# Unread identity products on TensorE, in nine places at both ends of a stack of four graph layers

## The chip, the cores and the metric

The kernel runs on one core of a Trainium2 chip. The core has five engines with their own instruction queues: TensorE (PE in the profile, with its weight loads shown apart as PEld), VectorE (DVE), ScalarE (ACT), GpSimd (POOL) and SyncE (SP), which here issues the transfers. Each engine works through its queue in order and waits on semaphores for the others. The metric is the device time of one execution in microseconds (us), lower is better.

## The reference

A batch of 32 graphs, each of 512 nodes with 256 features and a 0/1 adjacency matrix of 512x512, goes through four layers. After every layer comes a residual sum and a layer normalisation.

```python
x = _layernorm(x + layer0(x, adj))   # attention with 4 heads, relu, per-head normalisation
x = _layernorm(x + layer1(x, adj))   # attention with 1 head, elu
x = _layernorm(x + layer2(x, adj))   # transformer block: 8 heads, feed forward of 1024
x = _layernorm(x + layer3(x, adj))   # attention with 1 head, leaky relu

# a graph attention layer (3):
Wh = jnp.einsum('bnf,of->bno', h, W)
e = (Wh @ a1)[:, :, None] + (Wh @ a2)[:, None, :]
e = jnp.where(e > 0, e, ALPHA * e)
e = jnp.where(adj == 0, NEG_INF, e)
h_prime = jnp.einsum('bij,bjo->bio', jax.nn.softmax(e, axis=2), Wh)

# layer 2
scores = jnp.einsum('bhqd,bhkd->bhqk', q * scale, k)
attn = jax.nn.softmax(jnp.where(allowed[:, None], scores, -jnp.inf), axis=-1)
x = _layernorm(x + heads_joined(attn @ v) @ Wo.T + bo, ln1_g, ln1_b)
x = _layernorm(x + jax.nn.relu(x @ W1.T + b1) @ W2.T + b2, ln2_g, ln2_b)
```

## The kernel before

All 512 nodes of a graph lie as 4 rows of 128 partitions (R = 4, P = 128); the 256 features are 2 blocks of 128 (K = 2). Every layer is a Python generator that hands back control with `yield` between small pieces of work, called units here: one unit is, for example, the transposes of one feature block, the projection of one row, or the products of one attention row. `paced` (line 111) drives the generator of a stage and gives every unit a due time from the table `PLACES`, plus 12054 (`PERIOD`) times the graph's number. `graph` strings the stages of one graph together, and a merge of the 32 graphs by due time (line 832) sets the order in which the units are written out. So units of graph 0 stand beside units of graph 1, and in the steady part about four graphs are in work at once.

On TensorE this order is taken as written (`manual_schedule` for PE, line 831). For DVE, ACT and SP the framework's planner sets the order when the program is built: it goes through the instructions with estimates of their durations, hands out the buffers and banks that are free, and adds the waits.

All results of TensorE go to one pool of 8 PSUM banks (`bank`, in the pool `ps`), each 128x512 in float32. A bank is free again once it was read. Buffers named `part` (9 of them in stage "a") hold gb, pt and scratch tensors.

The units that matter here, with the names of the profile:
- layer 0: h0p (projection), gp (transposed broadcast of exponentials, copied to gb by ACT, line 349), then for each of four j: four pt on DVE (line 407), o and den on PE; then back on ACT (464), backp on PE, and a chain of DVE and ACT operations (lines 493 to 496, 293 to 302, and `layernorm`, lines 273 to 280) that ends with y on ACT (line 280).
- layer 1: xt1p (transposes of y, line 318 on), xt on ACT (line 320), h1p (projection), gp, gb, four pt, o in four rows, each by `attend`.
- layer 2: xt2p, qkp, hi (ACT, line 559) and lo (DVE, line 560), which are spread over partitions by transfers (line 567); s and pr, cp, den, ct (line 611), the projection wop, then a normalisation, ytp, f1p, ft (ACT, line 706), f2p, and two normalisations.
- layer 3: xt3p, h3p, gp, gb, pt, o in four rows, and the last normalisation.

Every matrix product is recorded by the helper `product`, so all have line 104 in the profile, and are told apart by their tensors. Between the units the kernel has no work for PE beyond what the merge places there; at the start only graph 0 and then graph 1 are under way, and at the end only graphs 30 and 31.

In weight preparation, `weights_ff` adds a loaded vector ln1b on DVE (line 227). The transfers of weights are issued on SP in the first 27 us.

The tensor `identb`, a bfloat16 identity of 128x128, is there already: it is multiplied with the mask `shut` in the products s<-shut,identb.

Of the kernel before, what the change touches and what calls it, by code (L numbers as in the profile page):

```python
# [44 lines left out]
        39499, 39646, 39646, 40873, 41200, 41449, 41464,  # L45
    ],
    "layer 3": [44919, 44919, 44969, 44969, 44969, 44969, 45682, 48065, 48065, 48065, 48422, 48422],
}
STAGES = {"edges": "a", "x": "a", "layer 0": "a", "layer 1": "a", "feed forward": "c", "layer 3": "c"}
ALL = mybir.DependencyInfo(mybir.DependencyClass.Sync, mybir.DependencyReason.DATA)  # L50
# [6 lines left out]
def tile_gnn_stack(tc: tile.TileContext, a: dict, out: bass.AP):  # L57

    nc = tc.nc
    with tc.tile_pool(name="verdict", bufs=1) as pool:
        bad = pool.tile([1, 1], I32, name="bad")
        fast_path(tc, a, out, bad)
        failed = nc.values_load(bad[0:1, 0:1])
        with tc.If(failed > 0):
            general_path(tc, a, out)
# [3 lines left out]
def fast_path(ctx: ExitStack, tc: tile.TileContext, a: dict, out: bass.AP, bad: bass.AP):  # L73
# [8 lines left out]
    nc = tc.nc  # L82
    B, N, D = a["x"].shape
    P = 128
    R = N // P
    K = D // P
    H, _, HO = a["w0"].shape
# [15 lines left out]
    def product(what, *args, **kwargs):  # L103
        latest[0] = what(*args, **kwargs).ins.name  # L104

    def in_place(op):

        if latest[0]:
            tc.add_manual_dep(op.ins, latest[0], ALL, reason="in its place")

    def paced(b, name, units):

        i = 0
        while True:
            stage[0] = STAGES.get(name, "b")
            try:
                next(units)
            except StopIteration as end:
                return end.value
            yield PERIOD * b + PLACES[name][min(i, len(PLACES[name]) - 1)]  # L120
            i += 1
# [4 lines left out]
    identb = const.tile([P, P], BF16, name="identb")  # L126
# [126 lines left out]
    def bank(name, dtype=F32):  # L253
        shape = [P, 2048 // (2 if dtype == BF16 else 4)]
        return ps.tile(shape, dtype, tag="mm", name=name, bufs=8)
# [546 lines left out]
    def graph(b):  # L802
        yield PERIOD * b + PLACES["edges"][0]
        rd = sb.tile([P, ND], F32, tag="rd", name="rd", bufs=3)
        mvs = sb.tile([P, 2 * NL * R + H * R + 2 * K], F32, tag="mvs", name="mvs", bufs=3)
        mv = [mvs[:, 2 * i * R : 2 * (i + 1) * R].rearrange("p (r s) -> p r s", s=2) for i in range(NL)]
        tops = mvs[:, 2 * NL * R :]
        var, spread = tops[:, : H * R], tops[:, H * R :]
        rds = [rd[:, ends[i] : ends[i + 1]] for i in range(3)]
        if b == 0:  # L810
            xt, x = yield from paced(b, "x", load_x(b))
        at = yield from paced(b, "edges", mask(b))
        if b:
            xt, x = yield from paced(b, "x", load_x(b))
        x = yield from paced(b, "layer 0", layer0_all(b, x, xt, at, rds[0], mv, var))
        x = yield from paced(b, "layer 1", layer1_all(b, x, at, rds[1], mv))
        a2 = yield from paced(b, "mask", symmetric(b, at))
        qk = yield from paced(b, "qkv", qkv_all(b, x))
        ct = yield from paced(b, "attention", attention(qk, *a2, spread))
        y = yield from paced(b, "projection", attended_all(b, x, ct))  # L820
        x = yield from paced(b, "feed forward", feed_forward_all(b, x, y, mv))
        x = yield from paced(b, "layer 3", layer3_all(b, x, at, rds[2], mv))
        nc.sync.dma_start(out[b].rearrange("(r p) d -> p r d", p=P), x)
        okd, oks, okv = ok[:, :ND], ok[:, ND : ND + NL * R], ok[:, ND + NL * R :]
        nc.vector.scalar_tensor_tensor(okd, rd, RD_MIN, okd, op0=ALU.is_ge, op1=ALU.mult)
        nc.vector.scalar_tensor_tensor(okd, rd, RD_MAX, okd, op0=ALU.is_le, op1=ALU.mult)
        variances = mvs[:, 1 : 2 * NL * R : 2]
        nc.vector.scalar_tensor_tensor(oks, variances, VAR_MAX, oks, op0=ALU.is_le, op1=ALU.mult)
        nc.vector.scalar_tensor_tensor(okv, tops, VAR_MAX, okv, op0=ALU.is_le, op1=ALU.mult)
# [12 lines left out]
    p = bank("badp")  # L842
# [651 lines left out]
```

## Time and profile before

| | |
|---|---|
| median of 3 runs | 3497.07 us (3495.69 to 3497.55) |
| profiled execution: its time | 3497.4 us |
| profiled execution: its span | 3495.6 us |
| mean granted clock of TensorE over the span | 0.986 |
| PE busy | 3397.5 us (97%) |
| PEld busy | 2366.5 us (68%) |
| DVE busy | 2888.4 us (83%) |
| ACT busy | 2223.0 us (64%) |
| POOL busy | 82.0 us (2%) |

Busy time is the time in which an engine executes, as the profiler records it; the ends of matrix products are modelled, so records of neighbours overlap, and the distance from start to start says what one costs in a row. The granted clock is the share of full speed at which TensorE was clocked; the profile gives it for every stretch of time. A group of instructions is written as out<-in with partitions x elements; "mean" is the duration of one. A float32 product shows two records in PE's timeline: a product of 256 float32 columns is two passes.

PE's waits and the chain of waits name the instruction that ended a wait last.

### The profile page before, as it was taken

Reading aid. Unit: us, or ns where it says so; the run is one execution under the profiler, and the core shown is the slowest. Engines: PE = TensorE matmul, PEld = TensorE weight load, DVE = VectorE, ACT = ScalarE, POOL = GpSimd, SP = SyncE. Lnnn points to the kernel's source line nnn. Section 1 sums busy time; section 2 is a strip of 40 time slices with the busy share of each in tenths; the row PEclk is TensorE's granted clock in tenths of the full one; section 3 lists DMA queues with packets and bytes.
Section 4 is the critical chain, followed back from the end, with each engine's and each line's share of the span. In section 5 each row is a group of like instructions: output and inputs, shape, how many; then the busy total and the mean of one; then the engine's idle time right before and its main releaser. Section 6 shows DMA issues by size and latency. Waiting matters only on the chain.

```text
span 3495.6 us, 51507 instructions
## 1 busy us (share of the span) xinstructions
PE 3397.5 (97%) x18342; PEld 2366.5 (68%) x18342; DVE 2888.4 (83%) x5178; ACT 2223.0 (64%) x5729; POOL 82.0 (2%) x171
## 2 busy tenths in 40 slices
PE   5799999999999999999999999999999999999986
PEld 3466667776667776667776667776666776666765
DVE  5778888888888888889888889888889888889863
ACT  3556667666667666667666667666667666666652
POOL 0000000000000000000000000000000000000000
PEclk8899999999999999999999999999999999999998
DMA  4334232333232333232333232334332333332220
GB/s 131 85 76 91 61 85 59 81 79 91 62 84 61 79 79 91 64 85 61 76 79 91 67 82 63 74 79 91 69 80 66 71 79 91 71 79 61 45 55 13
DMA packets 164038, 261.01 MB, mean 75 GB/s; under 512 B 20416, under 2 KB 56384, under 8 KB 163776
## 3 DMA queue, kind: packets, MB, share of 16 engines
q1 hardware_dynamic: 163776, 257.65, 32.0%
q8 instruction: 148, 2.42, 0.3%
q14 instruction: 114, 0.93, 0.1%
HBM read 106.57 MB, written 16.78 MB: 35 GB/s over the span
## 4 chain that ended last, share of the span: by engine, by line
PE 94%; DVE 3%; ACT 1%; issue 1%; DMA 1%; SPq 0%; POOL 0%; DVEq 0%; ACTq 0%; POOLq 0%
PE o L104 20%; PE f2p L104 13%; PE f1p L104 13%; PE s L104 8%; PE qkp L104 6%; PE cp L104 6%; PE den L104 5%; PE h3p L104 4%; PE wop L104 3%; PE h1p L104 3%; PE vp L104 3%; PE h0p L104 3%; PE gp L104 2%; PE backp L104 1%; PE xt3p L104 1%
## 5 line engine op out<-in xcount | busy, mean ns | idle before, releaser
L636 DVE TENSOR_TENSOR pr<-pr,a 128x1024 f32<-128x1024 f32 x384 | 454.7, 1217 | 185.4 <-ACT pr L633 185.4
L407 DVE SCALAR_TENSOR_TENSOR pt<-gb,ex,at 128x512 f32<-128x512 f32 x768 | 536.7, 742 | 42.0 <-ACT gb L349 31.6
L633 ACT ACTIVATE pr<-s 128x512 f32<-128x512 f32 x1024 | 545.3, 616 | 3.0 <-PE s L104 3.0
L104 PE MATMUL f2p<-wf,ft 128*128 128x256 f32 x2048 | 484.8, 379 | 5.4 <-ACT ft L706 5.2
L104 PE MATMUL f1p<-yt,wf 128*128 128x256 f32 x2048 | 483.8, 379 | 0.0
L104 PE MATMUL o<-h,pt 128*128 128x257 f32 x2048 | 476.5, 382 | 4.5 <-DVE pt L407 4.4
L104 PEld LDWEIGHTS o<-h,pt 128*128 128x128 f32 x2048 | 386.4, 190 | 99.1 <-issue 44.2
L663 DVE TENSOR_TENSOR pr<-pr 128x1024 f32<-128x1024 f32 x384 | 446.8, 1208 | 2.8 <-PE cp L104 2.8
L104 PEld LDWEIGHTS f2p<-wf,ft 128*128 128x128 f32 x2048 | 383.9, 190 | 63.4 <-ACT ft L706 9.8
L104 PEld LDWEIGHTS f1p<-yt,wf 128*128 128x128 f32 x2048 | 388.5, 190 | 55.0 <-DVE lo L560 0.5
L280 ACT ACTIVATE y<-y,rs 128x256 f32<-128x256 f32 x768 | 398.0, 593 | 17.1 <-DVE rs L276 17.1
L104 PE MATMUL s<-qk 128*128 128x512 f32 x1024 | 377.4, 470 | 4.6 <-DMA qk<-lo 3.8
L706 ACT ACTIVATE ft<-f1p,cols 128x256 f32<-128x256 f32 x512 | 217.0, 469 | 236.6 <-PE f1p L104 235.6
L273 DVE BATCH_NORM_STATS2 bn<-y 128x6 f32<-128x256 f32 x768 | 298.9, 410 | 5.6
L104 PE MATMUL o<-pt,hv 128*32 128x512 f32 x2048 | 286.5, 607 | 8.0 <-DVE pt L407 8.0
L265 ACT ACTIVATE rs<-mvs,eps1e-05_70 128x4 f32<-128x4 f32 x192 | 57.5, 300 | 326.7 <-DVE mvs L274 319.6
L104 PE MATMUL qkp<-xt,wqkv 128*128 128x512 f32 x512 | 240.5, 603 | 0.0
L104 PE MATMUL cp<-pr,v 128*32 128x512 f32 x2048 | 234.2, 595 | 1.4 <-DVE pr L636 1.4
L104 PEld LDWEIGHTS s<-qk 128*128 128x128 f32 x1024 | 189.3, 192 | 55.8 <-issue 27.7
L104 PEld LDWEIGHTS o<-pt,hv 128*32 128x32 f32 x2048 | 73.3, 110 | 179.6 <-issue 94.1
L559 ACT ACTIVATE hi<-qkp,cols 128x512 fp32r<-128x512 f32 x128 | 88.4, 691 | 164.1 <-PE qkp L104 162.1
L752 DVE RECIPROCAL rd<-o 128x1 f32<-128x1 f32 x128 | 21.5, 168 | 177.7 <-PE o L104 177.5
(139 smaller groups left out, 4881.9 us busy)
## 6 DMA issues: line engine op xcount, KB each, us to landing
qk<-hi SPq DMA_DIRECT2D x512, 128.0 KB, 3.4
qk<-lo SPq DMA_DIRECT2D x512, 128.0 KB, 3.5
adjt<-in_adjt SPq DMA_DIRECT2D x64, 512.0 KB, 3.9
adj<-in_adj SPq DMA_DIRECT2D x64, 512.0 KB, 5.0
xt<-in_xt SPq DMA_DIRECT2D x32, 512.0 KB, 3.8
x<-in_x SPq DMA_DIRECT2D x32, 512.0 KB, 5.1
out<-y SPq DMA_DIRECT2D x32, 512.0 KB, 4.5
wf<-in_w1t SPq DMA_DIRECT2D x1, 1024.0 KB, 9.8
```

Source lines behind the costliest of these rows:

```text
L104: latest[0] = what(*args, **kwargs).ins.name
L265: nc.scalar.activation(out, variance, AF.Ln, bias=eps[e])
L273: nc.vector.bn_stats(st[:, r, :], y[:, r, :])
L280: nc.scalar.activation(y[:, r, :], y[:, r, :], AF.Identity, bias=rs[:, 1, r : r + 1], scale=rs[:, 0, r : r + 1],)
L407: nc.vector.scalar_tensor_tensor(t, g, f, edges, op0=ALU.max, op1=ALU.mult)
L559: nc.scalar.activation(hi, p, AF.Identity, bias=bias)
L633: nc.scalar.activation(t[:, i, :], s, AF.Exp, scale=QSCALE)
L636: nc.vector.tensor_mul(t, t, edges)
L663: nc.vector.tensor_add(t, t, u)
L706: nc.scalar.activation(ft[:, f, :], p[:, f, :], AF.Relu, bias=bf1[:, ff + f : ff + f + 1])
L752: nc.vector.reciprocal(rd[:, r : r + 1], p[:, D : D + 1])
```

## The change

Before chosen units, `keep_busy` writes n products of `identb` with `identb` repeated four times, 128x512 in bfloat16, into a newly taken PSUM bank. Nothing reads the bank. The table `BUSY` is keyed by stage and unit (unit i is the piece that the i-th call of `next` runs, counted from 0), and then by graph: 0 and 1 are the first two, -2 and -1 the last two of the 32.

```diff
+BUSY = {
+    ("layer 0", 9): {0: 16, 1: 6},
+    ("layer 1", 1): {0: 72, 1: 40},
+    ("layer 1", 8): {0: 4},
+    ("layer 3", 1): {-2: 42, -1: 45},
+    ("projection", 1): {-1: 8},
+    ("layer 3", 8): {-1: 4},
+}
...
+    def keep_busy(n):
+        if n:
+            p = bank("busy").rearrange("p (r n) -> p r n", n=P)
+            for _ in range(n):
+                product(nc.tensor.matmul,
+                    p, identb, identb.unsqueeze(1).to_broadcast([P, R, P]), start=True, stop=True
+                )
+
     def paced(b, name, units):
 
         i = 0
         while True:
             stage[0] = STAGES.get(name, "b")
+            keep_busy(BUSY.get((name, i), {}).get(b if 2 * b < B else b - B, 0))
             try:
                 next(units)
```

Unit 9 of layer 0 is the first of the four j: its o products wait for pt. Unit 1 of layers 1 and 3 is the first block of transposes, xt1p or xt3p. Unit 8 of both is the first attention row, o. Unit 1 of the projection is the first row of wop. The products stand on PE directly ahead of these, 237 in all, in nine places; everything that follows on PE stands behind them.

## The prediction

> **What bounds the kernel now.** I read the slices of the page first, then the busy time per stretch, then PE's waits and PE's timeline at both ends, and last the granted clock in steps of 1 us.
>
> ```profile
> PE   5799999999999999999999999999999999999986
> PEclk8899999999999999999999999999999999999998
> ```
> ```profile
> 0.00:100.00 100.00, 64.50 (x324) 35.09 (x328) 58.77 (x100) 37.29 (x101) 4.68 (x16) 0.85 0.42 127
> 100.00:200.00 100.00, 79.68 (x408) 44.34 (x400) 73.14 (x113) 48.85 (x120) 2.96 (x5) 0.87 0.42 88
> ...
> 2000.00:2100.00 100.00, 100.00 (x552) 69.50 (x552) 86.61 (x159) 64.91 (x170) 2.49 (x5) 1.00 0.33 78
> ...
> 3400.00:3496.00 96.00, 66.70 (x274) 50.82 (x272) 31.96 (x93) 30.64 (x90) 0.00 (x0) 0.86 0.04 12
> ```
> The columns are stretch, length, busy us of PE, PEld, DVE, ACT and POOL, granted clock, DMA share, GB/s. From about 300 to 3300 us PE is busy without a break at clock 1.00: there the change can win nothing. But as that part is PE in a fixed order, every us by which PE reaches it earlier moves the end. The ends run at 0.85 to 0.87, and PE idles there. PE's waits of the first 250 us and from 3380 us on, each "waiter <- releaser: total, times, longest":
>
> ```profile
> PE xt1p L104 <- ACT y L280: 25.9, 2, 16.4
> PE o L104 <- DVE pt L407: 10.0, 6, 4.4
> ```
> ```profile
> PE xt3p L104 <- ACT y L280: 20.1, 2, 10.4
> PE wop L104 <- DVE ct L611: 2.5, 1, 2.5
> ```
> Four long waits are for a layer normalisation, a serial chain of DVE and ACT. After each of them PE works at half clock.
>
> **When the clock falls.** In steps of 1 us it changes at 19.56, 26.40, 43.46, 60.52, 67.36, 70.77, 84.42 and 87.84 us: the distances (6.84, 17.06, 17.06, 6.84, 3.41, 13.65, 3.42) are multiples of 3.41. So I cut the time into these windows:
>
> ```profile
> 57.11:60.52 3.41, 3.38 (x10) 2.19 (x11) 0.24 (x1) 1.98 (x4) 0.00 (x0) 0.50 0.00 0
> 60.52:63.94 3.42, 3.03 (x14) 2.28 (x12) 0.00 (x0) 1.47 (x4) 0.00 (x0) 1.00 0.00 0
> 63.94:67.36 3.42, 1.55 (x8) 1.00 (x8) 1.80 (x3) 0.91 (x4) 0.10 (x1) 1.00 0.00 0
> 67.36:70.77 3.41, 3.41 (x9) 2.47 (x8) 1.11 (x3) 0.75 (x2) 0.00 (x0) 0.50 0.00 0
> ...
> 118.54:121.96 3.42, 2.13 (x14) 0.53 (x16) 3.42 (x5) 2.42 (x5) 0.00 (x0) 1.00 0.89 173
> ...
> 139.03:142.44 3.41, 2.54 (x8) 1.29 (x7) 1.21 (x2) 3.41 (x8) 0.00 (x0) 0.50 0.00 0
> 142.44:145.86 3.42, 3.16 (x7) 2.52 (x8) 2.29 (x3) 1.06 (x3) 0.00 (x0) 0.50 0.01 2
> ```
> Each row decides the clock of the next. With 1.55 us of PE work (63.94) it falls, with 2.13 (118.54) it stays, with 3.38 (57.11) it rises; 2.54 us of transposes (139.03) do not raise it. [...]
>
> **The price of a product.** 237 bfloat16 products of 128x512 are added, each with its weight load. Nearest row: the pairs of an s product and a bfloat16 s<-shut of 128x512 take 0.46 us, and two s products alone also 0.46; so 0.23 us each at full clock. [...] The weight load (0.096 us on PEld) lies under the product before it. Each batch takes one of eight PSUM banks and is given back by PE itself: nothing, below by no more than one eviction (about 0.6 us, an ACT copy) for each of the nine batches, that is 0 to 5 us; I take 0, since in the waits the older banks are long read.
>
> **Place by place** (PE's timeline; PE is in order, so a product can only delay what follows it).
>
> *Graph 0, layer 0, 16 products* (3.5 us) in the 4.38 us before o at 21.04. PE then is warm and ends the first rows some 2 us earlier. But DVE's last four pt run at 32.95 to 35.7 behind the addition of ln1b, which waits for its DMA (landed 32.6, issued at 25.82, the queues full with weights). PE was already waiting for these pt. Gain 0; 2.4 at most if the addition gets another place in DVE's order.
>
> *Graph 0, layer 1, 72 products*: from 40.1 to 55.7 or 56.7. The last ACT y ends at 57.92, so the four transposes of k=0 end at about 58.1 in either case. The copies of xt (0.58 us) start at 58.3 and 58.84 instead of 58.49 and 59.34. h1p is 16 passes of 0.216 us warm (f1p: 8 in 1.73); seven pairs follow the second copy: 59.45 + 3.03 = 62.5 instead of 63.55. **1.0 us.**
>
> *Graph 0, layer 1, 4 products* (0.9 us) in the 1.55 us before o. The window holds 1.55 + 0.9 = 2.45 us and stays warm. The first row is paced by pt (0.68 us each, last ready at 68.3), ends at 68.8; three more of 1.73: 74.0 instead of 75.4. **1.3 us.**
>
> *Graph 1, layer 0, 6 products* (1.3 us) in the 2.19 us before 83.63: window 1.22 + 1.3 = 2.5. The last of four pt is ready at 85.5, o done at 85.9, den at 86.7 instead of 88.6. DVE's next pt waited 2.16 us for a buffer that den frees, so it moves too. **1.9 us.** The chain behind it (qkp, hi, the qk transfers, DVE from 113 to 137) hangs on PE and moves with it.
>
> *Graph 1, layer 1, 40 products* from 129.3, in 9.53 us. [...] The copies of xt stand behind four pr on ACT until 142.05, so xt1p may start as late as 141.0: 11.7 us of room. Then h1p warm: 3.46 instead of 5.31. **1.85 us.** If the cover were short, each 0.3 us of overrun costs 0.3.
>
> *Graph 30, layer 3, 42 products*: 9.1 to 9.7 us from 3386.85; the gap is 9.75, plus 1.4 up to the last y at 3398.02. h3p ends at 3402.4 instead of 3404.4. den and the ct of graph 31 stand behind it on PE: **2.0 us.** *Graph 31, projection, 8 products* (1.8 us) between den and wop, where PE waits 2.47 us for ct. wop x14 warm is 3.03 instead of 4.91: **1.9 us**; the o behind it (5.2 us) and ytp follow directly, and y's normalisation ends before them.
>
> *Graph 31, layer 3, 45 products*: 9.7 to 10.4 us in 10.36 plus 1.4. h3p ends 3.03 us after the second copy, which comes 0.1 earlier than 3469.43 + 0.58: 3472.4 instead of 3475.1. **2.7 us.** *The last 4 products* before o at 3477.4, where the clock was 1.00 already: 0; they keep it, should the window fall otherwise.
>
> Sum 1.0 + 1.3 + 1.9 + 1.85 + 2.0 + 1.9 + 2.7 = 12.7 us. Against it: between the end of the four long batches and h1p or h3p only transposes run for some 3 us. [...] By the rule a window lying in that stretch drops the clock, and the gain of the place is gone; I put it at one in four for each of four places: 0.25 x (1.0 + 1.85 + 2.0 + 2.7) = 1.9. By the busy rows alone it would be 0. I take it: **gain 10.8 us.** The profiled execution took 3497.4 (span 3495.6), the median is 3497.07, so 3486.6 and 3486.3: **3486.5 us.** What a measurement of this kernel can tell from no change is about 0.2%, 7.0 us.
>
> **The rivals.**
> *The clock falls again* at all four long waits. Left are 1.3 + 1.9 + 1.9 = 5.1 us: 3492, within 0.2%. For it: the transposes. Against it: their bursts are short, and a window must lie just so.
>
> *The order of the other engines shifts.* PE's order is written down, that of DVE, ACT and SP is made when the program is built, with the added products in its reckoning. In the steady part DVE is busy 85%; if one wait like that of o for pt at 172.0 (0.63 us) came back in each of some 30 graphs, 19 us are lost and 10.8 gained: 3505, slower. It decides from 0.36 us a graph on. For it: all graphs share buffers and banks, and nine more banks are handed out. Against it: the steady part has no wait now, DVE has 15 us of slack in 100, and nothing is added there.
>
> [...]
>
> **How the numbers follow.** Forecast 0.60 (its own range 3481 to 3490), clock falls again 0.20, order shifts 0.15, cold 0.05. Slower gets 0.12 of the shifted order and the cold 0.05: 0.17. Same gets 0.18 of the fallen clock and 0.03 of the shifted order: 0.21. Faster gets the forecast and 0.02 of the fallen clock: 0.62. Range 3480 (12.7 + 2.4 and some) to 3499 (5 us of bank waits or a small shift, set against the small gain): outside it are the cold case, most of the shifted order and a few hundredths below.
>
> **What would show it.** Clock 1.00 through 44 to 90 us and 3388 to 3475; h1p and h3p means near 390 ns instead of 435 to 557; PE's wait for y reduced to a rest; DVE's pt at 33 us still behind ln1b; the steady rows still 100.00. It is wrong if the rows between 300 and 3300 lose PE work, if busy products last over 0.23 us at clock 1.00, or if xt1p and xt3p start later than their y.

## The result, and the profile after

The kernel with the products takes 3490.23 us (median of 20 runs, 3488.44 to 3491.37); the kernel before, beside it, 3496.72 us (20 runs, 3493.08 to 3501.1). The ratio is 0.9981, with a 95% interval of 0.9974 to 0.9988: 6.5 us less, 0.19%. The forecast was 10.8 us less, 3486.5 us. The profiled execution took 3491.36 us, with a span of 3489.5 us (before: 3497.4 and 3495.6).

The 40 slices of the page, PE's busy share and the granted clock:

```profile
PE   7899999999999999999999999999999999999997
PEclk9999999999999999999999999999999999999999
```

Busy time per stretch, with the columns of the prediction (stretch, length, busy us of PE, PEld, DVE, ACT, POOL, granted clock, DMA share, GB/s):

```profile
0.00:100.00 100.00, 82.08 (x430) 42.40 (x434) 59.09 (x100) 37.40 (x101) 4.68 (x16) 0.98 0.42 128
100.00:200.00 100.00, 88.12 (x444) 47.68 (x440) 72.88 (x112) 48.87 (x120) 2.95 (x5) 0.93 0.42 87
2000.00:2100.00 100.00, 100.00 (x550) 69.52 (x549) 85.44 (x158) 65.57 (x172) 2.46 (x5) 1.00 0.33 80
3400.00:3489.00 89.00, 71.25 (x323) 50.90 (x321) 31.93 (x93) 29.70 (x85) 0.00 (x0) 0.97 0.04 13
```

The clock rose from 0.85, 0.87 and 0.86 to 0.98, 0.93 and 0.97 at the two ends; the middle is unchanged at 100.00 and 1.00. A higher mean clock is not yet time won: much of it lies over products that nobody reads, and what counts is how long the work behind each batch takes.

PE's waits of the first 250 us, and then from 3370 us on ("waiter <- releaser: total us, times, longest"):

```profile
PE xt1p L112 <- ACT y L297: 1.9, 7, 0.9
PE o L112 <- DVE pt L424: 5.9, 7, 2.2
PE h1p L112 <- ACT xt L337: 1.9, 2, 1.6
```
```profile
PE xt3p L112 <- ACT y L297: 2.2, 8, 0.7
PE wop L112 <- DVE ct L628: 0.8, 1, 0.8
```

The waits for y, 25.9 and 20.1 us before, are filled down to a rest. Two lines are to be kept in mind: a wait of h1p for xt of 1.6 us, and one of o for pt of 2.2 us. Each turns out to hold a part of the missing gain.

The batches and the work behind them in PE's timeline of after (start, us, operation, count, idle time before and what ended it):

```profile
42.17 15.70 PE L112 MATMUL busy<-identb 128*128 128x512 bf16 x72
61.23 3.81 PE L112 MATMUL h1p<-w1g,xt 128*128 128x258 f32 x16 [0.24 <-ACT xt L337]
...
127.21 10.49 PE L112 MATMUL busy<-identb 128*128 128x512 bf16 x40
141.68 5.16 PE L112 MATMUL h1p<-w1g,xt 128*128 128x258 f32 x16 [1.64 <-ACT xt L337]
...
3397.81 3.81 PE L112 MATMUL h3p<-w3g,xt 128*128 128x258 f32 x16 [0.24 <-ACT xt L337]
3406.30 3.29 PE L112 MATMUL wop<-wo,ct 128*128 128x256 f32 x14 [0.84 <-DVE ct L628]
3464.64 3.81 PE L112 MATMUL h3p<-w3g,xt 128*128 128x258 f32 x16 [0.24 <-ACT xt L337]
```

The same groups in PE's timeline of before:

```profile
59.12 4.43 PE L104 MATMUL h1p<-w1g,xt 128*128 128x258 f32 x16
...
142.70 5.30 PE L104 MATMUL h1p<-w1g,xt 128*128 128x258 f32 x16 [1.07 <-ACT xt L320]
...
3399.22 5.19 PE L104 MATMUL h3p<-w3g,xt 128*128 128x258 f32 x16
3409.09 4.91 PE L104 MATMUL wop<-wo,ct 128*128 128x256 f32 x14 [2.47 <-DVE ct L611]
3469.21 6.02 PE L104 MATMUL h3p<-w3g,xt 128*128 128x258 f32 x16
```

A projection that records 3.81 us ran warm (clock 1.00, its passes 0.22 us apart from start to start), one of over 5 us cold for most of its length (clock 0.50, 0.43 us apart); for the 14 passes of wop it is 3.29 against 4.91. Graph 0 and the whole tail are warm now (3.81, 3.81, 3.29, 3.81). Graph 1 is not: 5.16 against 5.30.

**Where the time went**, from the starts of the same instructions in both profiles. The first h0p starts at 10.54 instead of 9.16, and backp at 40.70 instead of 38.46: the kernel is 2.24 us *later* before any long batch begins. Behind that point the places give back 0.75 (graph 0, layer 1), 1.25 (its 4 products), 1.2 (graph 1, layer 0), 0.15 (graph 1, layer 1), 1.55 and 1.6 (the h3p of graph 30 and the wop of graph 31), and 2.4 (the h3p of graph 31), and the 3200 us between head and tail drift by 0.1: 9.0 us in all. 9.0 - 2.24 = 6.8 us, and PE's last product (badp) starts 6.78 us earlier, at 3480.72. The span is only 6.1 us shorter, since from the issue of the last output transfer to the end it takes 6.7 us instead of 6.0.

One place that neither kernel fills has a part in every such comparison. Ahead of the h3p of graph 29 (start 3310.55 in before, 3309.32 in after) PE waits 1.4 us for y, and in ten of the fourteen profiles of this case, before and after among them, the clock is at a half there for 3.41 us; in four (without products, half the products, bf1p moved, the addition alone) it is not. That is worth about 1.1 us.

In order of instructions ACT and POOL have the same as before, PE the same apart from the products. DVE differs in one place: one of the last pt of graph 0, layer 0, now stands ahead of the addition of ln1b.

Three things were open: why graph 1's h1p stayed cold, what the late start of the first 40 us is, and which batches earn their place.

### The profile page after: what moved, and what is told of

Its sections match the earlier page's. It is cut to its first block, busy times and chain, and to the rows that moved or that the text cites. A ratio compares the mean times of both kernels' runs of the same rounds, so it can differ in the third digit from the quotient of the medians.

```text
span 3489.5 us, 51983 instructions
## 1 busy us (share of the span) xinstructions
PE 3436.7 (98%) x18579; PEld 2383.9 (68%) x18579; DVE 2889.2 (83%) x5178; ACT 2222.6 (64%) x5729; POOL 81.7 (2%) x171
## 4 chain that ended last, share of the span: by engine, by line
PE 94%; DVE 3%; ACT 1%; issue 1%; DMA 1%; SPq 0%; POOL 0%; ACTq 0%; DVEq 0%; POOLq 0%
PE o L112 20%; PE f2p L112 13%; PE f1p L112 13%; PE s L112 8%; PE qkp L112 6%; PE cp L112 6%; PE den L112 5%; PE h3p L112 3%; PE h1p L112 3%; PE wop L112 3%; PE vp L112 3%; PE h0p L112 3%; PE gp L112 2%; PE backp L112 1%; PE xt3p L112 1%
```

## The experiments

Theory and rivals to begin with: the gain is the sum of the warm projections, about 3 us at the head and 6 at the tail, less what the start loses (theory); or head and tail are of another size than the profile says, because the head's loss belongs to the products and the tail's gain to luck (rivals). Every ratio is against "before", run in the same group. The intervals are some 3 us to either side, so a difference of 1 or 2 us between two changed kernels is not shown by the times alone. Line numbers shift a little between kernels.

**Head and tail apart.** One kernel keeps the batches of graphs 0 and 1 (138 products), the other those of graphs 30 and 31 (99).

```diff
 # head only
     ("layer 1", 8): {0: 4},
-    ("layer 3", 1): {-2: 42, -1: 45},
-    ("projection", 1): {-1: 8},
-    ("layer 3", 8): {-1: 4},
```
```diff
 # tail only
-    ("layer 0", 9): {0: 16, 1: 6},
-    ("layer 1", 1): {0: 72, 1: 40},
-    ("layer 1", 8): {0: 4},
     ("layer 3", 1): {-2: 42, -1: 45},
```

> Only the five batches of graphs 0 and 1 (138 products); the four of graphs 30 and 31 are left out. Theory (gain is where the clock no longer falls, and adds up): the two profiles give the head 1.15 us net, after 3.45 us won at xt1p, o and den of graphs 0 and 1 and 2.24 lost ahead of backp, of which 1.38 were already there at the first product and may be chance; so 1 to 2.5 us under before, 3494 to 3496. Rival (the start of the profile before was a lucky one, and the head wins all of 3.45 and more): 3.5 to 5 us under before.

> Only the four batches of graphs 30 and 31 (99 products). Theory: h3p of graph 30 1.55, wop 1.6, h3p of graph 31 2.4, together 5.6 us under before: 3491. Rival (the tail overlaps with DVE and part of it is taken back in the last normalisation): under 3.5 us.

Measured: head 3495.58 us (13 runs) against 3496.52, ratio 0.9994 (0.9986 to 1.0003); tail 3492.48 us (21 runs), ratio 0.9989 (0.9982 to 0.9995). So 0.9 and 4.0 us, together 4.9 where the change has 6.5; the intervals allow the two to add up. The head's interval includes no change at all; it excludes a gain of 5 us. The tail, costed at 6.6 us in the prediction before the discount, is under the 5.55 us that the profile of after shows. Its own profile shows what may be missing: there the h3p of graph 31 took 5.44 us, not 3.81. The same batch, with the same work behind it, is warm in one execution and cold in another.

**The addition of ln1b on GpSimd.** In after, PE waits 2.23 us for a pt on DVE, and that pt stands behind the addition, which waits for its transfer:

```profile
34.66 0.42 DVE L244 TENSOR_TENSOR b_b<-b_b,ln1b 128x256 f32<-128x256 f32 x1 [2.20 <-DMA ln1b<-in_ln1b]
```
```profile
35.80 2.78 PE L112 MATMUL o<-pt,hv 128*32 128x512 f32 x10 [2.23 <-DVE pt L424]
...
40.70 1.64 PE L112 MATMUL backp<-ident,back 128*128 128x128 f32 x12 [0.69 <-ACT back L481]
```

The first fence is DVE's timeline, the second PE's. The experiment takes the addition off DVE, so that no pt stands behind the transfer.

```diff
         bcast(ln1b, "ln1b")
-        nc.vector.tensor_add(lnb2, lnb2, ln1b)
+        nc.gpsimd.tensor_add(lnb2, lnb2, ln1b)
```

> All 237 products, and the addition of ln1b moved from DVE's queue to GpSimd's. Theory (the first 16 products win nothing because DVE's last pt of graph 0 stand behind an addition that waits for a weight transfer): the wait of 2.2 us for pt goes, backp starts 2 to 3 us earlier against the first product, the time is 2 to 3 us under the changed kernel. Rival (the start as a whole is later because transfers landed later, the addition only shows it): within 1 us of the changed kernel, and another wait for a transfer ahead of backp.

Measured: 3488.84 us (13 runs), ratio 0.9977 (0.9968 to 0.9985): 1.4 us under the change by the medians, which the intervals of the two alone don't separate. PE's timeline shows the mechanism, though:

```profile
36.21 1.63 PE L112 MATMUL backp<-ident,back 128*128 128x128 f32 x12 [0.69 <-ACT back L481]
```

backp starts 26.15 us after the first h0p (10.06), in after 30.16 us. The wait for pt of 2.2 us is gone. That less than those 4 us reaches the end is in part the clock's doing: in this profile the h1p of graph 0 took 4.87, that of graph 1 6.74 and the h3p of graph 31 5.49 us.

**Seven products more, before h1p of graph 1.** In graph 1 the copies of xt stand behind four pr on ACT, as the prediction said; so PE ends its batch at 137.7 and has only eight transposes until h1p at 141.7, 4 us. Two windows of 3.41 us from the trace of after:

```profile
137.73:141.14 3.41, 1.75 (x8) 0.94 (x8) 0.92 (x1) 3.41 (x9) 0.00 (x0) 1.00 0.00 0
141.14:144.55 3.41, 2.87 (x7) 2.31 (x8) 2.58 (x3) 1.35 (x4) 0.00 (x0) 0.50 0.01 2
```

1.75 us of PE work, nearly all of it transposes, and the next window has 0.50. The edit fills the wait between the transposes and the projection:

```diff
     ("layer 1", 8): {0: 4},
+    ("layer 1", 3): {1: 7},
```

> All 237 products and 7 more in graph 1 between the transposes xt1p and the projection h1p, in the 1.64 us in which PE waits for xt. Theory (the 40 products are spent for nothing because the clock falls after them, in a window that holds only transposes and this wait): clock 1.00 through h1p, h1p 3.8 us instead of 5.2, 1.4 to 1.7 us under the changed kernel. Rival (the stretch is bound by the copies on ACT, not by the clock): no gain over 0.3 us.

Measured: 3488.52 us (14 runs), ratio 0.9976 (0.9968 to 0.9984), by the medians 1.7 us under the change, which the intervals again don't separate. PE's timeline:

```profile
139.69 1.67 PE L113 MATMUL busy<-identb 128*128 128x512 bf16 x7
141.49 3.81 PE L113 MATMUL h1p<-w1g,xt 128*128 128x258 f32 x16
```

h1p starts when it did (141.49 and 141.68) and takes 3.81 us. So most of the gain which the prediction had given to the 40 products needed these seven too. In five profiles with the 40 products and without these seven, h1p took 5.15 to 6.81 us, never 3.81.

**The products out again, and the change a second time**, one run each: is the late start due to the products, and does a second execution of the change look like the first?

```diff
-BUSY = {
-    ("layer 0", 9): {0: 16, 1: 6},
...
-}
+BUSY = {}
```

> The changed source with an empty table of batches: no product at all, the same instructions as the kernel before. One look at the start: in the two profiles without products in graphs 0 and 1 the first h0p began at 9.2 us, in the four with them at 10.1 to 10.5, because the transfer of a landed later. Theory (chance of the transfers' start): anywhere from 9 to 10.6. Rival (the longer program delays the first transfers): 9.1 to 9.4.

> The changed kernel once more, for a second profile. Theory (free windows): h3p of graph 31 and h1p of graph 0 are warm (3.8 us) in some executions and partly cold (5.4, and about 4.5) in others, h1p of graph 1 is cold always. First h0p: by chance anywhere from 9 to 10.6; by the rival 10 to 10.6.

Measured: 3495.95 us without, with h0p at 9.17 as before; 3491.49 us for the change, with h0p at 10.85 and backp at 41.35. The h1p of graph 0 and both h3p were warm again, the h1p of graph 1 cold again (6.80).

**Half the products** in the four long waits: 36, 20, 21 and 22 (the expectation has 23 for the last). If some activity anywhere in the wait is enough, half is as good as all.

```diff
-    ("layer 1", 1): {0: 72, 1: 40},
+    ("layer 1", 1): {0: 36, 1: 20},
...
-    ("layer 3", 1): {-2: 42, -1: 45},
+    ("layer 3", 1): {-2: 21, -1: 22},
```

> The four long batches cut to half (36, 20, 21, 23 products), the five short ones as in the change. Theory (a batch is worth something only if it reaches up to the next work, as the clock falls in any window left idle): the clock falls in all four long waits, xt1p, h1p, xt3p and h3p are cold again, the 0.75 + 1.55 + 2.4 us of these places are lost: 4 to 5 us over the changed kernel. Rival (the products keep the clock for longer than a window, half of them would do): within 1 us of the changed kernel.

Measured: 3493.03 us (12 runs), ratio 0.9995 (0.9986 to 1.0003), 2.8 us over the change by the medians, less than the 4 to 5 expected. PE's timeline:

```profile
40.26 7.93 PE L112 MATMUL busy<-identb 128*128 128x512 bf16 x36
56.83 2.81 PE L112 MATMUL xt1p<-ident,y 128*128 128x128 f32 x8 [8.64 <-ACT y L297]
...
3395.89 4.64 PE L112 MATMUL h3p<-w3g,xt 128*128 128x258 f32 x16
```

In this profile the clock fell in all four waits (53 to 63, 124 to 131 and again 138 to 145, 3391 to 3398, 3459 to 3466 us; the fall at 124 is before the batch), and rose again only while the projections ran: they took 4.64 to 5.43 us, between the cold and the warm time. (The times from 124 to 145 us and at 3391 are an estimate, from the steps of 3.41 us and from what ran there: 20 products in 6.02 us, h1p in 5.35, h3p in 4.64.) That "between" may be why the loss was smaller than expected; the profiled execution, 3490.70 us, is the fastest of the twelve, so it can't tell what the median lost. In this profile what counts is that the products reach up to the next work, not that there are some.

**Everything at once, and one product between transposes.** In the profile of the run with the addition on GpSimd, the stretch ahead of the cold h3p looks like this:

```profile
3458.86:3462.27 3.41, 2.35 (x11) 1.35 (x12) 0.00 (x0) 2.83 (x6) 0.00 (x0) 1.00 0.00 0
3462.27:3465.68 3.41, 3.41 (x9) 2.69 (x9) 0.00 (x0) 1.33 (x8) 0.00 (x0) 0.50 0.00 0
```

PE is recorded busy for 2.35 us, more than the 2.13 us with which the clock stayed up at 118.54 in the kernel before. But here much of it is transposes of 128x128 in float32. (The row holds the eight transposes, 1.76 us, and three passes of h3p.) If transposes count less than products, a product between them is what is missing. The kernel has the change, the addition on GpSimd, the seven products, and in the long waits one product after each of the first three transposes of the first feature block:

```diff
     ("layer 3", 8): {-1: 4},
+    ("layer 1", 3): {1: 7},
 }
+BETWEEN = {("layer 1", 1): (0, 1), ("layer 3", 1): (-2, -1)}
...
                 )
+                if spare[0] is not None and r < R - 1:
+                    keep_busy(1, spare[0])
             nc.scalar.copy(t[:, k, :], p)
```

> The change, the addition of ln1b on GpSimd, 7 products before h1p of graph 1, and one product after each of the first three transposes of xt1p and xt3p in the four long waits, where PE waits for y anyway. Theory (transposes alone let the clock fall): clock 1.00 from there through h1p and h3p of all four graphs in every profile; gains of ln1b (1.5) and of h1p of graph 1 (1.7) add up, and the cold h3p of graph 31 and h1p of graph 0 go too (1.6 and 0.7 in about half of the executions): 4 to 5 us under the changed kernel, 3485 to 3486.5. Rival (more products only delay the transposes): 3487 to 3489.

Measured: 3484.95 us (6 runs) against 3496.58, ratio 0.9966 (0.9954 to 0.9978): 11.6 us under before. All four projections took 3.81 us. The end of the last long wait in PE's timeline:

```profile
3457.63 0.33 PE L114 MATMUL xt3p<-ident,y 128*128 128x128 f32 x1 [0.65 <-ACT y L307]
3457.79 0.38 PE L114 MATMUL busy<-identb 128*128 128x512 bf16 x1
...
3459.10 0.77 PE L114 MATMUL xt3p<-ident,y 128*128 128x128 f32 x5
3460.10 3.81 PE L114 MATMUL h3p<-w3g,xt 128*128 128x258 f32 x16 [0.24 <-ACT xt L349]
```

The products stand in the 0.16 us in which PE waits for the next y, and cost the transposes nothing that can be seen. One profile can't show that the clock never falls there; behind the batches it did not in this one, nor in that of the kernel with bf1p moved below. No run has the products between the transposes alone: by the medians they are what is left of 5.3 us under the change after 1.4 and 1.7 for the other two edits.

**The first 16 products**, taken out alone, and left alone. By the prediction they are worth nothing, 2.4 us at most. One rival made them the cause of the late start (A), another gave them a gain that the late addition hides (B).

```diff
 # without them
-    ("layer 0", 9): {0: 16, 1: 6},
+    ("layer 0", 9): {1: 6},
```
```diff
 # they alone
-BUSY = {
-    ("layer 0", 9): {0: 16, 1: 6},
...
-}
+BUSY = {
+    ("layer 0", 9): {0: 16},
+}
```

> The change without its first batch (16 products ahead of o in graph 0). Theory (that batch wins nothing, as DVE's pt wait for the addition of ln1b and so for a transfer): within 0.7 us of the changed kernel. Rival A (the batch is what delays the first transfers): first h0p at 9.1 to 9.3 us instead of 10 to 10.8, 1 to 2 us under the changed kernel. Rival B (the batch works as intended): 2 to 3 us over it.

> Only the first batch of 16. One look at the start: by rival A of the run before the first h0p begins at 10 to 10.8 us, else at 9.1 to 9.3. backp comes 29.3 us after the first h0p in the kernel before and 30.2 in the changed one; by the theory 29 to 30.5 here, by rival B 26.5 to 27.5.

Measured without them: 3491.2 us (14 runs) against 3497.07, ratio 0.9981 (0.9973 to 0.9989), that of the change; this alone would leave room for 2 to 3 us. h0p starts at 10.86: A falls. backp comes 29.16 us after it, with them 30.16: no sign of B in these two. With them alone 3496.11 us in one run, h0p at 10.70 and backp 27.28 us later, where before has 29.30: neither the 29 to 30.5 of the theory nor quite nothing. One number goes with both. In this profile the transfer of ln1b had landed early by the kernel's own clock (the addition starts 22.22 us after h0p, in after 24.12), and then the earlier rows of o are worth something. The distance from the addition to backp is nearly fixed: 5.85 us in before, 5.86 without the 16, 5.06 with them alone, 5.07 in the head alone, and 6.04 in after, where the clock falls in the wait (half clock from 35 to 39 us). So in these profiles backp follows the landing of the transfer, and the 16 products move the distance by less than 1 us to either side.

**bf1p moved.** In before and in every kernel so far the clock also falls between 190 and 197 us (in before at 193.6), with PE busy without a break. There stand the 32 passes of bf1p, of one column each. They, and the load of their weights wf1, go into the long wait of graph 1, two products after each four passes; the batch there shrinks from 40 to 8 and 16 of these. The rest is the kernel above.

```diff
-    ("layer 1", 1): {0: 72, 1: 40},
+    ("layer 1", 1): {0: 72, 1: 8},
...
+            if (name, i, b) == ("layer 1", 1, 1):
+                bias_ff()
...
-    def weights_ff():
-
+    def bias_ff():
         load_w(wf1, "w1t")
...
                 )
+            keep_busy(2, spare[0])
         nc.vector.tensor_add(bf1, bf1, p[:, :, 0])
```

> As the run with products between the transposes, and the 32 passes of bf1p (weights alone, 4.0 us on PE, after which the clock falls for 3.4 to 6.8 us at 193) go into the long wait of graph 1, mixed with 16 products, in place of 32 of the 40 there; w1's load moves ahead with them. Theory: PE loses 4 us of work and 1.7 to 3.4 us of half clock at 190 to 200, and the wait of 10 us takes it all: 5 to 7 us under the run with products between the transposes, about 3478 to 3480. Rival (the mixture doesn't hold the clock, so h1p of graph 1 is cold again, 1.7 us, and the batch is longer than the wait): 0 to 4 us under it.

Measured: 3478.01 us (5 runs, 3477.22 to 3478.77) against 3497.07, ratio 0.9946 (0.9932 to 0.9959): 19.1 us under before and 12.2 under the change. PE's timeline in the wait:

```profile
128.19 0.59 PE L114 MATMUL bf1p<-cols,wf 128*128 128x1 f32 x4
128.64 0.59 PE L114 MATMUL busy<-identb 128*128 128x512 bf16 x2
```

And the stretch where bf1p stood, first in before and then here:

```profile
190.00:200.00 10.00, 10.00 (x52) 6.00 (x54) 5.21 (x17) 1.65 (x4) 0.00 (x0) 0.68 0.92 164
```
```profile
190.00:200.00 10.00, 10.00 (x58) 6.27 (x57) 6.33 (x10) 5.66 (x12) 0.00 (x0) 1.00 0.84 143
```

From 0.68 to 1.00, with PE busy the whole time in both. Against the kernel with the products between transposes, the start of graph 1's h1p is 1.2 us earlier (138.34 and 139.54) and that of graph 30's h3p 8.05 us (3385.21 and 3393.26): 6.85 us come from between. Of these 3.96 are the passes themselves (in before 190.51 to 194.47), and 1.5 are won from 191 to 197 us, where the clock no longer falls. But 1.05 come at the h3p of graph 29, which is cold in the one profile (4.84 us) and warm in the other (3.81): by chance, as far as is known. The remaining 0.35 is a slow drift over the steady part. The 1.2 us ahead of all this, which stand by 35 us, stay open; that the load of 1 MB leaves the first 27 us is a guess.

**The addition on GpSimd alone**, without any product: is the late start the products' doing, and what is the addition worth by itself?

```diff
-BUSY = {
-    ("layer 0", 9): {0: 16, 1: 6},
...
-}
+BUSY = {}
...
-        nc.vector.tensor_add(lnb2, lnb2, ln1b)
+        nc.gpsimd.tensor_add(lnb2, lnb2, ln1b)
```

> No products; the addition of ln1b on GpSimd alone. Theory (without the products PE works cold there and is about as late as the transfer, so the addition costs little; it only takes what the first batch would win): 0 to 0.7 us under the kernel before. Rival (the addition's wait costs its 1 to 2 us with or without products): 1 to 2 us under it. The first h0p: 9.1 to 9.3 us if the late start belongs to programs with products in graphs 0 and 1, as in all nine such profiles so far; over 10 if it is chance.

Measured: 3495.7 us (13 runs) against 3496.34, ratio 0.9997 (0.9989 to 1.0005). The two expectations, up to 0.7 and 1 to 2 us under before, are not told apart by this. But backp comes 27.06 us after the first h0p, in before 29.30: against its reason, the addition's wait costs some 2 us there without any products too. h0p starts at 10.48, with no product in the kernel: the late start needs no products. In the profiles without products at the head, before, the tail alone and the empty table, it was at 9.16 to 9.24; in ten with them at 9.66 to 10.97; and here at 10.48. With three and eleven profiles, whether it is chance or something in how a program is laid out stays open.

## Why the prediction was right, and where it was not

The mechanism was right: the waits are filled, the clock stays up at graph 0 and through the tail (1.00 from 39 to 100 and from 3375 to 3482 us), and the middle has lost nothing (PE 100.00 in 2000 to 2100). The time lies in the range, 3.7 us above the forecast and just past the 3481 to 3490 of the forecast case itself. The range would also have held the rival of the fallen clock, 3492, so it is the profile that decides for the forecast, and not the time. 0.19% is just inside what the prediction called no change from the measurement; with 20 runs on each side the interval excludes 1. Term by term, by the profile of after:

| step of the prediction | us forecast | us measured |
|---|---|---|
| graph 0, layer 0, 16 products | 0 (2.4 at most) | none seen (3491.2 without them) |
| graph 0, layer 1, 72 | 1.0 | 0.75 |
| graph 0, layer 1, 4 | 1.3 | 1.25 |
| graph 1, layer 0, 6 | 1.9 | 1.2 |
| graph 1, layer 1, 40 | 1.85 | 0.15 |
| graph 30, layer 3, 42 | 2.0 | 1.55 |
| graph 31, projection, 8 | 1.9 | 1.6 |
| graph 31, layer 3, 45 | 2.7 | 2.4, about 0.8 where the clock falls |
| drift between head and tail | 0 | 0.1 |
| sum | 12.7 | 9.0 |
| the clock falls again | -1.9 | in the rows above |
| ahead of backp | 0 | -2.24 in this pair of profiles |
| behind the last product | 0 | -0.7 in this pair of profiles |

**The step that was mis-sized** is "one in four for each of four places". No run shows the rule that it goes by; what the runs show is how often each place lost the clock, and the chances are not alike. At graph 30 the h3p was warm (3.81 us) in all six profiles with the full batch and without a product between the transposes. At graph 31 it was cold (5.44 to 5.49) in three of six, at graph 0 the h1p partly cold (4.87 to 5.06) in three of six. At graph 1 it was cold (5.15 to 6.81) in all five: the prediction had read that xt stands behind four pr until 142.05, used it as "11.7 us of room" for the batch, and didn't add that the batch then ends 4 us ahead of h1p, with little but transposes between. The seven products confirm it: warm (3.81 us) in that profile, with nothing else changed on PE. But the five are not five free draws: counting in steps of 3.41 us from the clock's changes, in all of them a window began within 0.2 us of the batch's end. A stretch of 4 us need not hold a whole window, so "always" is not shown for another place of it. At graph 31 the traces show what the place does: in the three cold cases the window began between 0.2 us before and 0.3 us behind the end of the batch, in the three warm ones 0.4 to 0.8 us behind it, where it takes in more of h3p. Taken as one in one, a half, none and a half of 1.85, 1.0, 2.0 and 2.7, the term would have been 3.7 us instead of 1.9, and the gain forecast 9.0 instead of 10.8.

As much lies in **the gain of a warm projection**, which is too large at all five. The prediction counts a warm one by starts, 16 x 0.216 = 3.46 (or 14 x 0.216 = 3.03), and at four of them sets against it the end of the cold record, which for h1p of graph 1 gives 5.31. From the start to the start of the next product both are to be had: warm 3.64 (3397.81 to 3401.45 in after), cold 4.94 (142.70 to 147.64 in before). So 1.85 should have been 1.3, and 1.0, 2.0, 1.9 and 2.7 measured 0.75, 1.55, 1.6 and 2.4. The five are too large by 0.25 to 0.55 each, some 1.8 us together. The 6 products were too large by 0.7 besides.

**What was left out** is the start. The prediction priced the first 40 us at nothing, since pt waits for ln1b; that the wait sets backp is right. But the landing moves by a microsecond or two from profile to profile (the addition starts at 32.61 us in before, at 34.66 and 35.31 in the two profiles of the change), and so does the transfer of a, on which w and then h0p wait (the first operation on a starts at 6.83, 8.22 and 8.52); the median of 20 runs lies 2.5 us short of the 9.0. By the cold halves above, graphs 0 and 31 would give up some 0.6 + 0.8 of that on average (an estimate, half of what 4.87 to 5.06 and 5.44 to 5.49 are over 3.81; that both are warm in the profile of the table is luck). The rest fits a later start and a later end, but no profile shows them for the other 19 runs, and their cause is not settled.

**The price of a product.** 72 products took 15.70 us, the last of which lasts 0.39: (15.70 - 0.39) / 71 = 0.216 us each at full clock. The 0.23 that the prediction took from the row of the s products was too high. It cost nothing, as PE still waited 0.87 us for y behind the 72. The 40 products took 10.49 us, at half clock for 3.4 of them, where they start 0.43 us apart, inside the 11.7 us of room.

**Short gaps and transposes.** The 4 products in a gap of 1.55 us and the 6 in one of 2.19 us brought 1.25 and 1.2 us, so gaps this short do cost the clock here: in before it stands at 0.50 behind both, from 67.36 to 70.77 and from 84.42 to 87.84 us. The recorded busy time alone does not order what the clock did: 2.35 us of recorded work, 1.76 of it transposes, let it fall, 2.13 us without transposes, in before at 118.54, did not, and products between the transposes went with four warm projections (3.81 us each). That transposes count for less than products is one reading of this, and not shown. A rival to it stays untested: the record of a lone transpose lasts 0.33 us, but in a row they start 0.11 us apart, so the eight may be only some 0.9 us of work, and the row 1.5 instead of 2.35 (an estimate from these starts). Then it is the record that is too long, and a transpose need not count for less than a product. Products between the transposes help in either case.

**The rivals.** The order of the other engines did not shift, but for one pt at 32 us; the steady row stays at 100.00. The products, given 0.05 to run cold, ran at full clock, but for 3.4 us of the 40. "The clock falls again" came true at one place of four always and at two of them in half of the profiles.

## What to carry to other kernels

Filling a wait on TensorE paid here only by the work behind it: fill up to that work, through the transposes and the copies too (with seven products more the h1p of graph 1 took 3.81 us instead of 5.16, with half of the long batches the four projections took 4.64 to 5.43), and look at the first projection's duration, not at the mean clock. Where the clock changes in steps, of 3.41 us here, give a chance by the length of the thin stretch and by where the steps lie: here the stretch of 4 us lost the clock in five profiles of five, those of 3.0 to 3.5 us in six of eighteen. Compare like with like: starts with starts, or records with records. And look for real work to put into the wait: moving 32 thin passes there brought about as much, 7 us by the medians, as all 237 products.

## What the runs showed of the hardware that was not expected

Passes of one column let the clock fall although PE is recorded busy without a break: bf1p, 32 passes in 3.96 us, and clock 0.68 in the 10 us around and behind it. With two products of 128x512 after each four passes, in another place, the clock was back at 1.00 from about 128.4 us on and stayed there: over 120 to 140 us it is 0.83, which 6.8 us at a half give, and from 128.64 to 134.18 each pair of products starts 0.79 us after the one before (an estimate from these).

The clock changes in steps of 3.41 us (in after it falls and rises at 127.49, 130.91, 141.15 and 144.56 us: 3.42, 3 x 3.41 and 3.41 apart), and where the steps lie relative to the work differs from execution to execution: at the end of the last long batch by 1 us between the profiles. So the same batch is followed by warm and cold projections, 3.81 and 5.44 us for the h3p of graph 31, and no single profile gives the average.

The first product on TensorE, which waits through w on DVE for one of the first transfers, started between 9.16 and 10.97 us in the fourteen profiles, with the same transfers issued in the same order in all but the kernel with bf1p moved, which issues that of wf later than the others.
